# Attention's maxima in wider steps, and three scratch writes for four

## The chip, the cores and the metric

The kernel runs on one core of a Trainium2 chip. A core has five engines with their own instruction streams: TensorE (PE, matrix products and transposes into PSUM), VectorE (DVE), ScalarE (ACT), GpSimd (POOL) and SyncE (SP, which issues plain transfers). SBUF and PSUM are its two memories; sixteen DMA engines move data between SBUF and the chip's main memory. Indirect transfers (gathers of table rows by index) are issued from GpSimd's queue. The metric is the time of one execution on the device, in microseconds (us), as the median of several runs.

## The reference

A graph layer on 6250 nodes of 128 features and 200000 edges, sorted by their destination node. Everything is float32. `mesh_conv` gathers node rows, makes a message for every edge, and averages the messages by destination; attention follows:

```python
h = mesh_conv(x, src, dst, edge_attr, c1...)       # group norm, silu, segment mean
h = silu(group_norm(h)) + time embedding
h = mesh_conv(h, src, dst, edge_attr, c2...)
h = silu(group_norm(h)) + x
q, k, v = h @ qw + qb, h @ kw + kb, h @ vw + vb    # 8 heads of 16
logits = (q[dst] * k[src]).sum(-1) * scale + (edge_attr @ ew + eb)
amax = segment_max(logits, dst)
pe = exp(logits - amax[dst])
ssum = segment_sum(pe, dst)
o = segment_sum((pe / ssum[dst]) * v[src], dst)
return h + group_norm(o @ ow + ob)
```

## The kernel before

The edges are cut into 196 chunks of 1024 (eight tiles of 128 edges). There are three long stages: the two convolutions (`conv(1)`, `conv(2)`) and attention. Each walks the chunks once in `pipeline`, which writes out the order of the work. `in_order` pins that order on VectorE, ScalarE, TensorE and SyncE; GpSimd's order comes from its own issue order.

**Step n of attention's pipeline.** `fetch(n + 1)` issues the loads of the next chunk: SyncE loads the rows of the destination window (`pk`), and for every second chunk the positions from which the one-hot is made (`ohT`, 112 x 8 KB); GpSimd issues eight gathers (L622), one per tile, of 128 rows of keys and values (1 KB each) from `kv_d` into a buffer `g`. There are 11 such buffers. Then `second` finishes an older chunk, `first(n)` computes chunk n's logits, then some node work (`batch`, which finishes blocks of destination nodes that no further edge will touch) and `products(n + 1)`.

**First part.** `logits` multiplies the queries (`qe`, in PSUM, made by TensorE with the one-hot) with the gathered keys, tile by tile (L1187, three instructions), reduces over the head (L1190) and adds the edge term (L1192) into `lg`, which holds eight chunks.

**Maxima.** After eight chunks, a run, `maxima` makes the running maxima of the run. It is a generator with pieces, and between them the caller puts other work. Piece 1: transposes on TensorE of half of the logits (L1216, tile `lt`). Piece 2: the first forward scan on VectorE (L1219), then the transposes of the other half. Piece 3: the second forward scan, a backward scan over all 1024 edges (L1222), and transposes back (L1226, tile `rm`). Piece 4: the logits minus the maxima (L1230), the exponential on ScalarE (L1232), and eight products of the maxima with the end marks (L1234). The tiles `lt`, `rm` and the node work's `nd` share one place in PSUM.

**Second part.** For each chunk of the run before: the one-hot (`onehot`, L639), the late addition of the chunk before that into the table of sums (`add_late`, L1270 to L1276), the values weighted by the exponentials (`weighted`, L1244), the sums by destination on TensorE (`sums`, L1251), and `merge_late` (L1284 to L1262), which corrects the running maxima of the node windows. In the step in which a run has ended, the pieces of `maxima` stand between these; before the change: piece 1, one-hot, piece 2, late addition, piece 3, weighted product, sums, merge, piece 4, and then `first`.

**GpSimd's scratch writes.** After the eight gathers of a chunk, `gather` puts `REST[i]` memsets of a scratch tile `nst2` (128 x 392 elements, L634), which nothing reads: three in the convolutions, four in attention. The next chunk's gathers are issued behind them. Each gather also waits for the semaphore of the gather eight before it, and the first one of a chunk for its buffer.

Of the kernel before, what the change touches and what calls it, by code (L numbers as in the profile page):

```python
# [24 lines left out]
HD = 16  # L25
NT = 8
CH = NT * P
REST = {1: 3, 2: 3, 3: 4}
G = 8
GC = 2  # L30
BN = 4
# [14 lines left out]
def kernel(ctx: ExitStack, tc: tile.TileContext, x, src, dst, eat, w, out):  # L46
# [12 lines left out]
    NCH = EW // NT  # L59
# [538 lines left out]
    def loads(c, pools, rows_d, ahead):  # L598
        k = Chunk()
        k.c = c  # L600
        k.src, k.dm = src_i[:, c * NT:(c + 1) * NT], dm0[:, c * NT:(c + 1) * NT]
        if c == 0:
            load_group(0, pools)
        k.pk = pk[c % NPK]
        first = value(lo_i, c, SP, N - 1)
        nc.sync.dma_start(out=k.pk[:WN, :D], in_=rows_d[bass.ds(first, WN), :])
        g = c + (LG if ahead == 1 else 1)
        if g % LG == 0 and g < NCH:
            load_group(g, pools)
        k.ohT = pools[c // LG][:, c % LG, :]  # L610
        return k
# [8 lines left out]
    def gather(k, g, table_d, rest=0):  # L620
        def start(t):
            return nc.gpsimd.indirect_dma_start(  # L622
                out=g[:, t, :table_d.shape[1]], out_offset=None, in_=table_d,
                in_offset=bass.IndirectOffsetOnAxis(ap=k.src[:, t:t + 1], axis=0))

        with ExitStack() as es:
            if rested and rest:
                es.enter_context(tc.issue_after(rested.pop().ins))
            for t in range(NT):
                last = start(t)  # L630
        if rest:
            with tc.issue_after(last.ins):
                for _ in range(rest):
                    last = nc.gpsimd.memset(nst2, 0.0)  # L634
                rested.append(last)

    def onehot(k, pools, iota):
        k.oh = pools["oh"].tile([P, NT, P], FP, name="oh")
        return nc.vector.tensor_tensor(  # L639
            k.oh, iota[:, None, :].to_broadcast([P, NT, P]),  # L640
            k.dm[:, :, None].to_broadcast([P, NT, P]), ALU.is_equal)
# [322 lines left out]
    def conv(i):  # L964
# [4 lines left out]
        with ExitStack() as es:  # L969
# [73 lines left out]
            class Stage:  # L1043
# [4 lines left out]
                def fetch(self, c):  # L1048
                    k = loads(c, pools, a_d[i], self.ahead)
                    k.g = gp.tile([P, NT, D], FP, name="g")  # L1050
                    gather(k, k.g, b_d[i], REST[i])
                    k.h = hs[c % len(hs)]
# [5 lines left out]
                def first(self, k):  # L1058
                    if self.j == 0:
                        self.var = vp.tile([P, NV + BN * H], FP, name="var")  # L1060
                    k.reduce = first(k, self.var, self.j)
                    self.j += 1
# [60 lines left out]
            def left(k):  # L1123
                left_rows(k, pools, a_d[i], "m", [P, NT, D], 2)
                k.g = gp.tile([P, NT, D], FP, name="g")
                gather(k, k.g, b_d[i])
                k.h = hs[0]
                hidden(k, [(k.ohf.rearrange("p t e -> p (t e)"), k.rows[:, :D]), (k.ea, wcl)])
                var = vp.tile([P, NV + BN * H], FP, name="var")
                first(k, var, 0)()  # L1130
                nc.vector.reciprocal(rs_ps[:, :NT * H], deviations(NT * H, var)[:, :NT * H])
                k.rs = rs_ps[:, :NT * H]
                normed(k)
                summed(k)
                s = U[:, bass.ds(k.win, 1), :wide].rearrange("p o c -> p (o c)")
                nc.vector.tensor_tensor(s, s, k.u[:, :wide], ALU.add)
# [23 lines left out]
    with ExitStack() as es:  # L1160
# [21 lines left out]
        def logits(k, lg):  # L1182
            ebs = wk.tile([P, NT, H], FP, name="ebs")
            for a, qe in zip(range(0, NT, TB), k.qe):
                n = min(TB, NT - a)
                kk = k.g[:, a:a + n, :D]
                nc.vector.tensor_tensor(kk, qe[:, :n, :D], kk, ALU.mult)  # L1187
                nc.scalar.copy(ebs[:, a:a + n, :], qe[:, :n, D:])  # L1188
            l3 = wk.tile([P, NT, H], FP, name="l3")
            nc.vector.tensor_reduce(  # L1190
                l3, k.g[:, :, :D].rearrange("p t (h c) -> p t h c", c=HD), AX.X, ALU.add)
            nc.vector.tensor_tensor(lg, l3, ebs, ALU.add)  # L1192
# [46 lines left out]
        def weighted(k):  # L1239

            k.v = vp.tile([P, NT, VK + H + 1], FP, name="v")
            v4 = k.v[:, :, :VK].rearrange("p t (h c) -> p t h c", c=HD + 1)
            nc.scalar.copy(v4[:, :, :, HD], k.pe)
            nc.vector.tensor_tensor(  # L1244
                v4[:, :, :, :HD], k.g[:, :, D:].rearrange("p t (h c) -> p t h c", c=HD),
                k.pe[:, :, :, None].to_broadcast([P, NT, H, HD]), ALU.mult)

        def sums(k, wide):
            k.u = ps_.tile([P, 512], FP, name="u", tag="u", bufs=2)
            for t in range(NT):  # L1250
                nc.tensor.matmul(k.u[:, :wide], lhsT=k.oh[:, t, :], rhs=k.v[:, t, :wide],  # L1251
                                 start=(t == 0), stop=(t == NT - 1))
# [27 lines left out]
        def merge_late(k):  # L1280

            pres = k.u[:, VK + H:VK + H + 1]
            nm = wk.tile([P, 2], FP, name="nm")
            nc.vector.scalar_tensor_tensor(  # L1284
                nm, pres.to_broadcast([P, 2]), BIG, nm2[:, :, k.c], ALU.mult, ALU.add)
            cm = wk.tile([P, 2, H], FP, name="cm")
            nc.vector.tensor_tensor(
                cm, k.u[:, None, VK:VK + H].to_broadcast([P, 2, H]), nm[:, :, None].to_broadcast([P, 2, H]), ALU.add)
            k.win = value(w0_i, k.c, DVE, NW - 1)
            merge(k, M[:, bass.ds(k.win, 2), :], None, cm, 2)  # L1290

        def add_late(k):
            add(k, t3[:, bass.ds(k.win, 2), :], 2)

        class Stage:
            ahead = 1
            sums, late, nb = [], [], None
            lg, j = None, 0

            def __init__(self, bp):  # L1300
                self.bp = bp
# [3 lines left out]
            def fetch(self, c):  # L1305
                k = loads(c, pools, a_d[3], self.ahead)
                k.g = gp.tile([P, NT, KV], FP, name="g")
                gather(k, k.g, kv_d, REST[3])
                k.qe = []
# [5 lines left out]
            def first(self, k):  # L1315
                if self.j == 0:
                    self.lg = wk.tile([P, NT, G, H], FP, name="lg")
                logits(k, self.lg[:, :, self.j, :])
                self.j += 1

            def reduce(self, k):
                pass
# [5 lines left out]
            def second(self, run, ks):  # L1328


                pieces = iter(())
                if run:
                    pieces = maxima(run, self.lg, self.nb, self.bp)
                    self.nb, self.j = None, 0
                for n, k in enumerate(ks):
                    mine = pieces if n == len(ks) - 1 else iter(())
                    next(mine, None)
                    onehot(k, pools, iota)
                    next(mine, None)


                    if self.late:
                        add_late(self.late.pop(0))
                    next(mine, None)
                    weighted(k)
                    nc.scalar.copy(k.v[:, :, VK:VK + H], k.wl)
                    nc.scalar.copy(k.v[:, :, VK + H], ef[:, k.c * NT:(k.c + 1) * NT])
                    sums(k, VK + H + 1)
                    if self.sums:
                        merge_late(self.sums[0])  # L1350
                        self.late.append(self.sums.pop())
                    self.sums.append(k)
                for _ in pieces:
                    pass

            def batch(self, j):
# [95 lines left out]
```

## Time and profile before

| what | us |
|---|---|
| median of 3 runs (lowest to highest) | 7131.07 (7125.32 to 7133.75) |
| the profiled execution | 7126.42 |
| its span (first to last instruction) | 7124.6 |
| both convolutions, first to last gather | 56 to 4617 |
| attention, first to last gather | 4669 to 7051 |

The profile is of one execution. An engine's busy time is the sum of its instructions, without those that wait or only issue. A line of a group reads: line of the kernel, engine, operation, what is written from what, count, busy time, mean nanoseconds of one, and after the bar the idle time of the engine just before these instructions with what ended most of it ("issue" where nothing that the profile shows was waited for). In a timeline a line has the start, the length, the engine, the line and the operation; neighbours of one kind are merged, with their number, and the brackets hold the idle time before. In the table of stretches PEclk is the granted share of TensorE's clock.

### The profile page before, as it was taken

What the parts mean: (1) busy time and instruction counts of PE and PEld (TensorE: products, weight loads), DVE (VectorE), ACT (ScalarE), POOL (GpSimd) and SP (SyncE); (2) the same over time, 40 slices, a digit from 0 to 9 for tenths busy, and PEclk for the clock granted to TensorE, in tenths of its full rate; (3) what the DMA queues carried; (4) which work ended last, traced back from release to release, by engine and by line L of the source; (5) the groups of instructions that cost most, each with busy time, mean ns of one, the idle gap of its engine ahead of it and who ended that gap; (6) DMA issues with size and microseconds to landing.
All of it is one profiled execution on the core that took longest, in us unless ns stands there. A gap on an engine that the chain in (4) does not pass through costs nothing. (4 is left out here: it accounts for less than half of the span.)

```text
span 7124.6 us, 74065 instructions
## 1 busy us (share of the span) xinstructions
PE 3891.3 (55%) x20957; PEld 3685.5 (52%) x20958; DVE 5144.2 (72%) x7564; ACT 3308.5 (46%) x5293; POOL 5394.0 (76%) x6678
## 2 busy tenths in 40 slices
PE   5555555555555455555555555545555555555555
PEld 4555555555555455555555555535555555555554
DVE  7777777777777576667777777736667777777778
ACT  5555555555555555555555555522223333333332
POOL 5777777777777677777777777767777777777774
PEclk7776677777777666666777777767777777777777
DMA  5433333333333333333333333344455555555553
GB/s 148 117 97 91 94 110 92 100 100 100 95 100 89 91 90 94 95 94 89 101 107 106 100 106 106 86 130 132 131 146 140 141 142 140 141 146 141 138 139 89
DMA packets 414321, 800.44 MB, mean 112 GB/s; under 512 B 101813, under 2 KB 274984, under 8 KB 379496
## 3 DMA queue, kind: packets, MB, share of 16 engines
q0 software_dynamic: 175616, 411.34, 22.2%
q1 hardware_dynamic: 232646, 380.69, 19.0%
q10 hardware_dynamic: 5632, 3.51, 0.2%
q8 instruction: 172, 2.82, 0.2%
q14 instruction: 255, 2.09, 0.1%
HBM read 754.19 MB, written 40.96 MB: 112 GB/s over the span
## 5 line engine op out<-in xcount | busy, mean ns | idle before, releaser
L622 POOL DMA_INDIRECT g<-b_d,src_i x3136 | 3000.7, 957 | 978.7 <-issue 940.0
L1030 PE MATMUL u<-h,oh 128*128 128x129 f32 (+1 forms) x6272 | 1395.6, 412 | 1891.2 <-ACT h L1025 1891.2
L1030 PEld LDWEIGHTS u<-h,oh 128*128 128x128 f32 x6272 | 1290.1, 314 | 1971.5 <-ACT h L1025 1963.9
L622 POOL DMA_INDIRECT g<-kv_d,src_i x1568 | 1532.4, 977 | 500.9 <-issue 468.8
L1251 PE MATMUL u<-v,oh 128*128 128x145 f32 x3136 | 750.0, 425 | 767.2 <-DVE nm L1284 765.6
L1251 PEld LDWEIGHTS u<-v,oh 128*128 128x128 f32 x3136 | 698.5, 308 | 801.9 <-issue 801.9
L1000 PE MATMUL m<-pk,ohT 117*128 117x128 f32 x6272 | 973.7, 321 | 134.9 <-DVE h L1006 101.1
L1006 DVE TENSOR_TENSOR h<-m,g 128x1024 f32<-128x1024 f32 x392 | 479.0, 1222 | 762.3 <-DMA g<-b_d,src_i 750.4
L1000 PEld LDWEIGHTS m<-pk,ohT 117*128 117x128 f32 x6272 | 942.0, 237 | 162.1 <-DVE h L1006 126.9
L1025 ACT ACTIVATE h<-h 128x1024 f32<-128x1024 f32 x392 | 414.2, 1057 | 1182.9 <-DVE h L1024 1182.9
L634 POOL MEMSET nst<- 128x392 f32 x1960 | 842.7, 430 | 79.3
L1008 ACT ACTIVATE sq<-h 128x1024 f32<-128x1024 f32 x392 | 413.9, 1056 | 653.8 <-DVE h L1006 650.8
L1009 DVE TENSOR_REDUCE var<-sq 128x64 f32<-128x1024 f32 x392 | 477.7, 1219 | 314.8 <-ACT sq L1008 312.2
L1187 DVE TENSOR_TENSOR g<-qe,g 128x384 f32<-128x384 f32 (+1 forms) x588 | 293.8, 511 | 549.7 <-DMA g<-kv_d,src_i 510.1
L615 ACT ACTIVATE ohT<-ohT,minus_p 112x1024 f32<-112x1024 f32 x588 | 669.9, 1139 | 16.2 <-DMA ohT<-rel_d 16.0
L616 ACT ACTIVATE ohT<-ohT 112x1024 f32<-112x1024 f32 x588 | 621.4, 1057 | 18.7
L1178 PE MATMUL qe<-pk,ohT 117*128 117x136 f32 x3136 | 512.8, 319 | 165.5 <-ACT ebs L1188 159.3
L1178 PEld LDWEIGHTS qe<-pk,ohT 117*128 117x128 f32 x3136 | 474.1, 225 | 198.8 <-ACT ebs L1188 192.3
L1023 DVE TENSOR_TENSOR h<-h,cps 128x1024 f32<-128x1024 f32 x392 | 478.4, 1220 | 13.5
L1024 DVE TENSOR_TENSOR h<-h,cps 128x1024 f32<-128x1024 f32 x392 | 478.4, 1220 | 13.4
L1020 DVE TENSOR_TENSOR h<-h,cps 128x1024 f32<-128x1024 f32 x392 | 475.3, 1212 | 5.9
L639 DVE TENSOR_TENSOR oh<-cps,dm 128x1024 f32<-128x1024 f32 x392 | 475.9, 1214 | 0.0
(265 smaller groups left out, 4383.9 us busy)
## 6 DMA issues: line engine op xcount, KB each, us to landing
ohT<-rel_d SPq DMA_DIRECT2D x294, 896.0 KB
g<-b_d,src_i POOLq DMA_INDIRECT x3136
pk<-a_d SPq DMA_DIRECT2D x588, 56.0 KB
g<-kv_d,src_i POOLq DMA_INDIRECT x1568
ohT<-in_eat_dram SPq DMA_DIRECT2D x294, 40.0 KB
a_d<-n_o SPq DMA_DIRECT2D x28, 256.0 KB
kv_d<-n_o SPq DMA_DIRECT2D x28, 256.0 KB
n_h<-h_d SPq DMA_DIRECT2D x19, 256.0 KB
```

The source lines that it names most:

```text
L615: nc.scalar.activation(k.ohT[:WN, :], k.ohT[:WN, :], AF.Square, bias=minus_p[:WN])
L616: nc.scalar.activation(k.ohT[:WN, :], k.ohT[:WN, :], AF.Relu, bias=1.0, scale=-4.0)
L622: return nc.gpsimd.indirect_dma_start(out=g[:, t, :table_d.shape[1]], out_offset=None, in_=table_d, in_offset=bass.IndirectOffsetOnAxis(ap ...
L634: last = nc.gpsimd.memset(nst2, 0.0)
L1000: nc.tensor.matmul(k.m[:, t, :], lhsT=lhs[:, t * P:(t + 1) * P], rhs=rhs, start=(j == 0), stop=(j == len(terms) - 1))
L1006: nc.vector.tensor_tensor(k.mt, k.m, k.g, ALU.add)
L1009: return lambda: nc.vector.tensor_reduce(var[:, j * NT * H:(j + 1) * NT * H], sq.rearrange("p t (g c) -> p (t g) c", c=HD), AX.X, ALU.add)
L1023: nc.vector.tensor_tensor(k.mt, k.mt, over_edges(gam), ALU.mult)
L1024: nc.vector.tensor_tensor(k.mt, k.mt, over_edges(bet), ALU.add)
L1030: nc.tensor.matmul(k.u[:, :wide], lhsT=k.oh[:, t, :], rhs=k.h[:, t, :wide], start=(t == 0), stop=(t == NT - 1))
L1178: nc.tensor.matmul(qe[:, t, :], lhsT=lhs[:, e], rhs=rhs, start=(j == 0), stop=(j == len(terms) - 1))
L1251: nc.tensor.matmul(k.u[:, :wide], lhsT=k.oh[:, t, :], rhs=k.v[:, t, :wide], start=(t == 0), stop=(t == NT - 1))
```

## The change

Three things are changed, all in attention. The memsets after a chunk's gathers are three instead of four. The pieces of the maxima stand further apart: piece 2 comes after the late addition (before, ahead of it), and piece 3 after the sums (before, ahead of the weighted product). The last piece is kept and run by `first`, right behind the logits of the next chunk; for the very last run, which no chunk follows, it is run at once.

```diff
-REST = {1: 3, 2: 3, 3: 4}
+REST = {1: 3, 2: 3, 3: 3}
...
-            lg, j = None, 0
+            lg, j, pieces = None, 0, iter(())
...
             def first(self, k):
...
                 logits(k, self.lg[:, :, self.j, :])
                 self.j += 1
+                self.rest()
...
             def second(self, run, ks):
...
                     next(mine, None)
                     onehot(k, pools, iota)
-                    next(mine, None)
 
 
                     if self.late:
                         add_late(self.late.pop(0))
                     next(mine, None)
                     weighted(k)
...
                     sums(k, VK + H + 1)
+                    next(mine, None)
                     if self.sums:
                         merge_late(self.sums[0])
...
-                for _ in pieces:
+                self.pieces = pieces
+                if run and run[-1].c == NCH - 1:
+                    self.rest()
+
+            def rest(self):
+
+                for _ in self.pieces:
                     pass
```

The order that the program has after it, on VectorE, in the step in which a run ended: one-hot, late addition, first forward scan, weighted product, second forward scan, backward scan, merge, logits of the new chunk, subtraction L1230, the eight products L1234. On TensorE: transposes of the logits, sums, transposes back. On ScalarE the exponential stands behind the copies of the edge term. GpSimd's gathers are the same.

## The prediction

> **What bounds the kernel now.** I read the engine totals first, then the stage that the change touches, then who waits there.
>
> ```profile
> PE 3891.3 (55%) x20957; PEld 3685.5 (52%) x20958; DVE 5144.2 (72%) x7564; ACT 3308.5 (46%) x5293; POOL 5394.0 (76%) x6678
> ```
>
> No engine looks full. The busy sums of the two long stages (start, end, length; PE, PEld, DVE, ACT, POOL; clock, DMA share, GB/s) separate them:
>
> ```profile
> 56.00:4620.00 4564.00, 2508.09 (x13692) 2397.11 (x13691) 3329.58 (x3536) 2521.11 (x3121) 3510.90 (x4313) 0.72 0.37 99
> 4669.00:7051.00 2382.00, 1306.92 (x6804) 1216.58 (x6804) 1690.68 (x3749) 732.47 (x2045) 1866.27 (x2348) 0.72 0.51 139
> ```
>
> The second row is attention: POOL (GpSimd) is busy 78% and VectorE 71%. The grouped instructions of attention's middle, 5000 to 6800 us, say what POOL does in the rest:
>
> ```profile
> L622 POOL DMA_INDIRECT g<-kv_d,src_i x1181 | 1156.1, 979 | 365.4 <-issue 356.5 <-DVE g L1187 4.2 <-DVE wl L1234 3.3
> L634 POOL MEMSET nst<- 128x392 f32 x592 | 254.2, 429 | 25.6
> ```
>
> 1156.1 + 365.4 + 254.2 + 25.6 = 1801.3 us: the whole window. The idle part is 0.30 us ahead of each gather, put down to its own issue; buffers cost it some 9 us. The wait table of the same window has VectorE on the other side:
>
> ```profile
> DVE g L1187 <- DMA g<-kv_d,src_i: 353.9, 240, 4.2
> ```
>
> So gathers set the pace, and VectorE waits for them 354 us in 148 chunks, 2.4 us each. One period in the timeline of POOL:
>
> ```profile
> 5807.61 0.95 POOL L622 DMA_INDIRECT g<-kv_d,src_i  x1 [0.30 <-issue]
> ...
> 5817.30 1.89 POOL L634 MEMSET nst<- 128x392 f32 x4
> 5819.49 0.95 POOL L622 DMA_INDIRECT g<-kv_d,src_i  x1 [0.30 <-issue]
> ```
>
> 11.88 us from chunk to chunk: 8 gathers at 1.25 (10.0) and the four memsets with the issue after them (1.89). Nothing but POOL's own instructions is in it.
>
> **Part 1: one memset fewer.** A memset is 0.424 us and the gap to the next 0.058: 0.482 us a chunk. 196 chunks x 0.482 = 94.5 us. This is on the path as long as POOL waits for nothing. Three things could make it wait. (a) A free buffer: chunk 96's gather starts at 5831.38 into the buffer of chunk 85, whose last reader (L1244) ended at 5813.17, so 18.2 us are left; over all chunks in the trace the least is 13.7. (b) The landing of the gather eight before, since each gather waits for the semaphore of its slot. [...] The trace has 2.4 us for undisturbed gathers, but up to 7.9 from issue to landing where the one-hot's 896 KB load runs beside. [...] (c) VectorE: eight chunks take 8 x 11.89 + 2 = 97 us now and 91.3 after; VectorE waits for landings 19 us of each eight, so it needs 78 and keeps 13 over.
>
> The conv stages already run with three memsets, and their median period in the trace is 11.39 us, with gathers of 0.94 and memsets of 1.41 together. So POOL holds that period, though with rows half as long.
>
> Not all 196 pay. In the last chunks VectorE is late (chunk 190's products start 2 us after the last landing, 195's 6 us), so a faster gather there gives nothing: 6 chunks x 0.48 = 3 us, and a lead that it builds before that is spent there too; I take 6 us off, from 3 to 12.
>
> **Part 2: the scans move against the gathers.** The backward scan L1222 reads two SBUF operands. A gather that POOL starts inside it does not end until 0.76 us after it:
>
> ```profile
> 5838.70 2.28 DVE L1222 TENSOR_TENSOR_SCAN fw<-nbe,fw 64x1024 f32<-64x1024 bf16 x1
> 5838.88 2.86 POOL L622 DMA_INDIRECT g<-kv_d,src_i  x1 [0.30 <-issue]
> ```
>
> A gather that starts s us after the scan's start ends 3.04 us after that start, and loses 2.1 - s; one that started 0.05 us before a scan (at 5938.44, scan at 5938.49) took its usual 0.95. Of 26 scans 24 hit a gather, and their losses add up to 37.2 us. Memsets are not hit: at 7038.98 four of them take 1.88 us with a scan across them, and the gather behind them, 1.89 us into that scan, loses 0.2. [...]
>
> Where does the scan go? Now: one-hot, scan 1, late addition, scan 2, backward scan, weighted product. After: one-hot, late addition, scan 1, weighted product, scan 2, backward scan. One product (L1244 at 5840.90, the next start at 5842.02: 1.12 us) comes ahead of it. VectorE's clock is the landing of the chunk before, and POOL starts the next chunk 0.48 us earlier after that, so the scan falls 1.60 us later in the gathers' period: from 7.32 us (5838.70 - 5831.38) to 8.92. Gathers start at 8.75 and, after the memsets, at 11.41. The scan of 2.28 us then lies on the eighth gather's late part and on the memsets: no loss. Shifting all 26 scans by the same 1.60 leaves 10.8 us (8 of it in the first five runs, whose scans come earlier, at 6.5 to 7.0 us). Gain 26 us. But the eighth gather is only 0.17 us ahead: with a shift below 1.45 it is hit, and 29 to 35 us stay. Ends: 2 and 37; I take 26, since both terms are read from rows.
>
> **Part 3: the last piece behind the next logits.** The subtraction L1230 (0.68 us) and eight products L1234 (1.14 us) leave the stretch ahead of the landing and come after L1192; the exponential (0.60 us) goes with them on ScalarE. In that step VectorE is late by 1.0 to 2.3 us already; it becomes some 1 to 3 us later and starts the next step 1.8 us later. Behind it wait the next one-hot, the node work and, on TensorE, what uses the bank of the rm tile. VectorE's 2.4 us of slack per chunk takes it up in two steps; uncovered it would be 26 x 1.8 = 47 us. TensorE gains: the sums (4.2 us) run under the scans in place of waiting for the rm transposes, which had waited 4.45 us for L1222. On POOL's path: 0.
>
> **Part 4: node work's operations** (L795, L900, L902: all operands in SBUF, 0.69 us) cost gathers another 14.2 us now. The new period shifts them at random: 0, from -10 to +10.
>
> Sum: 94.5 - 6 + 26 = 114.5 us. The profiled execution had 7126.4 us (span 7124.6, so 1.8 lie around it), 4.7 below the median of the runs shown; 7131.1 - 114.5 = **7017 us**, 1.6% faster.
>
> **Rivals.**
> - *The scans still hit.* Only the memsets count: 94.5 - 6 - 2 = 86, **7045**. For it: a margin of 0.17 us. Against: none of the terms is guessed.
> - *The gain stops at VectorE or at landings.* If transfers crowd (51% of the DMA engines now, 53% after) and each landing comes later by most of the 0.48 us, POOL gains but VectorE gets its rows no sooner: 10 to 40 us, about **7105**. Against it: eighth gathers land 1.8 us after their end in nearly all chunks, with no growth within a chunk.
> - *Slower: VectorE becomes the bound.* Postponed pieces add waits on TensorE (the bank that lt, rm and nd share) until eight chunks take VectorE over 98 us. It decides from 19 us of added waits in each eight chunks; at 25 us a group of eight takes 104, and 24 groups x 6 us more give **7275**. Only 1.8 us is visible.
> - *Nothing happens*, if something not in the profile paces gathers and takes the memset's place: **7131**.
>
> **How the numbers follow.** The four parts as summed: 0.56 (own range 6995 to 7035). Scans still hit: 0.22. Stopped gain: 0.08, nothing: 0.03, slower: 0.11. About 0.2% (14 us) is what a measurement can tell from no change. Faster is 0.56 + 0.22 and 0.06 of the third: 0.84; same is 0.03 and the rest of the third: 0.05; slower 0.11. The range of 8 in 10 goes from 6985 (all 37 us won, node work better by 10) to 7095, which takes in the scans' rival with the larger tail loss and half of the stopped gain.
>
> **What would show it.** Right: POOL's timeline with three memsets of 1.41 us and 11.4 us from chunk to chunk; L622's mean for kv_d gathers near 0.95 in place of 0.979, L1222's start 0.1 to 0.3 us behind an eighth gather; VectorE's wait for gathers near 1.9 us a chunk. Wrong: L622's "issue" idle growing past 0.30, POOL waiting for L1244 or for a landing, gathers of 2 to 3 us beside L1222 still, or VectorE no longer waiting for gathers.

## The result and the profile after

| | before | after |
|---|---|---|
| median, us (lowest to highest) | 7130.9 (7125.32 to 7133.75), 4 runs | 7015.1 (7009.02 to 7021.43), 4 runs |
| ratio, with its 95% interval | | 0.9839 (0.9822 to 0.9856) |
| span of the profiled execution | 7124.6 | 7013.5 |
| first gather of attention starts | 4669.4 | 4671.8 |
| attention, first gather's start to last gather's end | 2381.7 | 2265.5 |
| from there to the end of the span | 73.5 | 76.1 |
| median period from chunk to chunk in attention | 11.892 | 11.415 |

The change saves 115.8 us of the median, and 7017 had been predicted. Of the 111.1 us in the span, attention gives 116.2, the tail takes back 2.6 and the convolutions, whose code is the same, 2.4.

This holds on the chip of this comparison and on one of the chips that the experiments ran on. On three others the kernel before takes 7327 to 7351 us. The changed kernel itself ran on one of these three and is 0.5% slower there; on the other two only parts and variants of it ran, and each of these with fewer than four writes is slower than the kernel before. The second half of the experiments is about that.

The engine totals of the changed kernel, as on the page:

```profile
PE 3856.5 (55%) x20957; PEld 3659.4 (52%) x20958; DVE 5143.7 (73%) x7564; ACT 3308.8 (47%) x5293; POOL 5285.4 (75%) x6482
```

POOL has 196 instructions fewer and 108.6 us less to do; VectorE's work is the same. The grouped instructions of attention's middle, 5000 to 6800 us, and VectorE's wait for gathers in that window (sum, count, longest):

```profile
L622 POOL DMA_INDIRECT g<-kv_d,src_i x1245 | 1195.8, 960 | 385.0 <-issue 369.7 <-DVE g L1187 6.9 <-DVE M L1262 3.0
L634 POOL MEMSET nst<- 128x392 f32 x468 | 201.8, 431 | 18.0
```

```profile
DVE g L1187 <- DMA g<-kv_d,src_i: 276.6, 212, 4.7
```

Gathers, memsets and the issue gaps again fill the whole window (1800.6 us), with 156 chunks in it for 148. The mean gather fell from 979 to 960 ns. The stalls, which are what gathers last beyond their usual 0.945 us, add up in this window to 10.4 us beside the backward scans (28.8 before) and 9.5 us beside other work (11.9 before). VectorE waits 1.77 us a chunk, where it waited 2.4 before. In the timeline of a step with the scans, the backward scan starts 0.31 us behind an eighth gather and lies across the memsets; none of them is longer for it:

```profile
5141.33 0.95 POOL L622 DMA_INDIRECT g<-kv_d,src_i  x1 [0.30 <-issue]
5142.59 0.94 POOL L622 DMA_INDIRECT g<-kv_d,src_i  x1 [0.30 <-issue]
5142.90 2.28 DVE L1222 TENSOR_TENSOR_SCAN fw<-nbe,fw 64x1024 f32<-64x1024 bf16 x1
5143.52 1.41 POOL L634 MEMSET nst<- 128x392 f32 x3
5145.23 0.95 POOL L622 DMA_INDIRECT g<-kv_d,src_i  x1 [0.30 <-DVE nm L1284]
```

### The profile page after: what moved, and what is told of

It reads as the page before. It is cut to its first block, busy times and chain, and to the rows that moved or that the text cites. A ratio compares the mean times of both kernels' runs of the same rounds, so it can differ in the third digit from the quotient of the medians.

```text
span 7013.5 us, 73893 instructions
## 1 busy us (share of the span) xinstructions
PE 3856.5 (55%) x20957; PEld 3659.4 (52%) x20958; DVE 5143.7 (73%) x7564; ACT 3308.8 (47%) x5293; POOL 5285.4 (75%) x6482
## 5 line engine op out<-in xcount | busy, mean ns | idle before, releaser
L622 POOL DMA_INDIRECT g<-kv_d,src_i x1568 | 1510.2, 963 | 500.9 <-issue 463.5
L1251 PE MATMUL u<-v,oh 128*128 128x145 f32 x3136 | 727.2, 415 | 755.7 <-DVE nm L1284 747.1
L1251 PEld LDWEIGHTS u<-v,oh 128*128 128x128 f32 x3136 | 675.1, 299 | 795.5 <-issue 795.5
L634 POOL MEMSET nst<- 128x392 f32 x1764 | 760.4, 431 | 67.9
```

What stands on the lines that cost most here:

```text
L622: return nc.gpsimd.indirect_dma_start(out=g[:, t, :table_d.shape[1]], out_offset=None, in_=table_d, in_offset=bass.IndirectOffsetOnAxis(ap ...
```

## The experiments

The experiments ran on four chips, here B to E, one after the other; A is the chip of the result above, of which no number is on record, so it may be C. Each kernel is compared with runs of the kernel before on its own chip. All versions do the whole computation.

| chip, kernel before (us) | version | median, us | ratio (95% interval) |
|---|---|---|---|
| A, 7130.9 | changed kernel | 7015.1 | 0.9839 (0.9822 to 0.9856) |
| B, 7351.3 | old pieces, three writes | 7501.6 | 1.0214 (1.0186 to 1.0241) |
| B | new pieces, four writes | 7341.3 | 0.999 (0.997 to 1.0009) |
| B | changed, last piece at once | 7384.6 | 1.0057 (1.0034 to 1.0079) |
| B | changed, no writes in attention | 7644.8 | 1.0403 (1.0379 to 1.0426) |
| C, 7132.2 | changed kernel | 7018.3 | 0.9841 (0.9825 to 0.9858) |
| C | old pieces, three writes | 7031.5 | 0.9859 (0.9843 to 0.9876) |
| C | changed, two writes | 6943.3 | 0.974 (0.9724 to 0.9756) |
| D, 7343.4 | changed, last piece at once | 7380.4 | 1.0059 (1.004 to 1.0078) |
| D | changed, one write | 7579.3 | 1.0321 (1.0276 to 1.0366) |
| D | changed, no writes in attention | 7631.2 | 1.0371 (1.0316 to 1.0426) |
| E, 7327.1 | changed kernel | 7361.0 | 1.005 (1.0025 to 1.0075) |

### One part at a time

The runs on chip B took the change apart. The write alone (the kernel before with three writes):

```diff
-REST = {1: 3, 2: 3, 3: 4}
+REST = {1: 3, 2: 3, 3: 3}
```

> One part alone: three memsets in attention, the pieces of the maxima where they were. Theory (GpSimd's instructions set the pace; a scan costs a gather 2.1 us less its offset): 196 x 0.48 = 94 us less, 6 lost in the tail; the scans move 0.48 us against the gathers, and the same shift of the 26 scans of before leaves 30 of their 37 us: 7036 us, chunk to chunk 11.41 us. Rival (the pieces carry the gain, the fourth memset hid behind something): within 30 us of 7131.

The pieces alone (the changed kernel with the fourth write back):

```diff
-REST = {1: 3, 2: 3, 3: 3}
+REST = {1: 3, 2: 3, 3: 4}
```

> The other part alone: the pieces apart, four memsets. Theory: the period stays at 11.89 us and the scans move 1.1 to 1.3 us, which leaves 27 to 31 of their 37 us: 7 to 10 us less, 7122 us. Rival (room between the pieces is what VectorE lacked): 30 us less or more, 7100 or below.

The changed kernel without the postponed piece:

```diff
                 self.pieces = pieces
-                if run and run[-1].c == NCH - 1:
-                    self.rest()
+                self.rest()
```

> The changed kernel, with the last piece of the maxima run at once behind the merge and ahead of the next logits, as before. Theory (VectorE's slack takes the last piece anywhere): 7015 us as changed, plus or minus 8, since only node work's place against the gathers moves. Rival (it must stand behind the logits, or VectorE's lateness reaches GpSimd): 26 x 1.8 = 47 us more, 7060.

And with no write in attention at all:

```diff
-REST = {1: 3, 2: 3, 3: 3}
+REST = {1: 3, 2: 3, 3: 0}
```

> The changed kernel with no memsets in attention. Theory: chunk to chunk 10.0 us; 196 x 3 x 0.48 = 282 us less, but each scan now hits a gather (26 x 1.5 = 39 us back from 18, so 20 lost), and VectorE needs 9.7 us a chunk, so some 20 to 40 us go in the tail: 6780 us. Rival (the memsets keep gathers from crowding something that the profile does not show): no gain below 7015, gathers that last over 0.95 us away from the scans, or waits of GpSimd for landings.

Only the pieces alone came out as expected in time: 10 us less, which the interval does not tell from no change. The reason given did not come out, as shown below, so the agreement is no support for it. Every version with fewer writes was slower than the kernel before; the version without writes missed its expectation by some 860 us. With a kernel before that was itself 3% slower than on chip A, the theory "GpSimd alone sets the pace" (theory A in what follows) had either fallen or was true on some chips only; theory B adds that TensorE has to deliver in time. So the changed kernel, the write alone and the kernel before (once, for its trace) ran on chip C, beside one step further:

> The changed kernel once more, beside the others of this call. Theory A, GpSimd alone paces attention: 110 to 120 us below the kernel before on the same chip, ratio near 0.984, whatever the chip. Theory B, GpSimd paces only as long as TensorE delivers in time: where the kernel before takes about 7130 us (granted clock near 0.723) the ratio is near 0.984; where it takes about 7350 us (granted clock near 0.694) the gain shrinks or turns, ratio 0.99 to 1.01, with VectorE waits for TensorE's results in attention and GpSimd waits for gather buffers, and attention takes 2300 to 2400 us for 2254.

> The old pieces with three scratch writes, once more. Theory A: 85 to 95 us below the kernel before, ratio near 0.987, on any chip. Theory B: near 0.987 where the kernel before takes about 7130 us; 1.015 to 1.03 where it takes about 7350 us, as in the first call. If it is slower on a chip where the kernel before takes about 7130 us, the cause lies in where the pieces stand and not in the chip.

> The kernel before, for its trace on the chip of this call. Theory A: chunk period of 11.9 us, attention 2370 us from the first gather to the last, GpSimd never waits for a buffer. Theory B: the same, since four scratch writes leave TensorE time; what waits for TensorE's results in attention stays under 20 us in sum even where the granted clock is near 0.69.

```diff
-REST = {1: 3, 2: 3, 3: 3}
+REST = {1: 3, 2: 3, 3: 2}
```

> The changed kernel with two scratch writes a chunk in attention for three. Theory A: another 0.48 us on 196 chunks, up to 94 us less than the changed kernel, of which the room of VectorE (78 busy of 91.3 us per eight chunks, now of 87.5) takes some: 20 to 90 us below it. Theory B: on a chip with a granted clock near 0.69 it is slower than the changed kernel by 20 to 150 us; near 0.72 it gains less than 40 us or loses.

On chip C the kernel before takes 7132 us (7135.7 in the profiled execution), and there theory A holds: the changed kernel gains 113.9 us, the write alone 100.7 (a little over the 85 to 95 expected, since it takes more of the scans' stalls away than expected), two writes 188.9. What the parts are worth there, from the traces (stalls as above; a scan's are those of the gathers that overlap it):

| | before | write alone | changed | two writes |
|---|---|---|---|---|
| median period, us | 11.902 | 11.420 | 11.418 | 10.927 |
| attention, us | 2386.8 | 2278.4 | 2263.9 | 2184.1 |
| stalls, scans', us | 39.3 | 28.6 | 14.8 | 28.8 |
| stalls, others', us | 16.8 | 13.3 | 12.6 | 13.1 |
| median start of the scan after its chunk's first gather, us | 7.30 | 8.04 | 9.07 | 9.60 |
| tail, us | 78.6 | 77.8 | 79.1 | 82.8 |

The write alone gives 0.482 x 195 = 94.0 us in the period and 14.2 in stalls; moving the pieces adds 14.5 us in attention (13.2 in the median). In the typical step of the write alone the scan starts inside the seventh gather and holds up the eighth:

```profile
5327.61 0.95 POOL L622 DMA_INDIRECT g<-kv_d,src_i  x1 [0.30 <-issue]
5328.11 2.28 DVE L1222 TENSOR_TENSOR_SCAN fw<-nbe,fw 64x1024 f32<-64x1024 bf16 x1
5328.86 2.29 POOL L622 DMA_INDIRECT g<-kv_d,src_i  x1 [0.30 <-issue]
```

The pieces alone, on chip B, put it 0.13 us ahead of the eighth gather's start in the step shown, and the gather takes 2.92 us, for 2.29 in the step above. 22 of 26 scans hit, and the stalls are 38.4 us, as much as in the kernel before (37.4 on A, 39.3 on C) and not the 27 to 31 us expected:

```profile
5533.66 2.28 DVE L1222 TENSOR_TENSOR_SCAN fw<-nbe,fw 64x1024 f32<-64x1024 bf16 x1
5533.79 2.92 POOL L622 DMA_INDIRECT g<-kv_d,src_i  x1 [0.30 <-issue]
```

So neither part alone moves the typical scan to where only memsets start inside it: the write moves it by 0.74 us in the median, the pieces by 1.30 (8.60 on B for 7.30 on C), and it takes both to pass the eighth gather's start at 8.77. With two writes the scan falls another 0.53 us later, the memsets are shorter (0.92 us in all for 1.41), and 24 of 26 scans hit gathers, most of them the next chunk's first ones. But the period follows the write, 0.49 us less, and that is worth more:

```profile
5312.52 0.95 POOL L622 DMA_INDIRECT g<-kv_d,src_i  x1 [0.30 <-DVE cm L1287]
...
5322.22 0.92 POOL L634 MEMSET nst<- 128x392 f32 x2
5323.44 0.95 POOL L622 DMA_INDIRECT g<-kv_d,src_i  x1 [0.30 <-DVE g L1187]
```

10.92 us from chunk to chunk, GpSimd waits for no buffer, and VectorE still waits for gathers (5000 to 6700 us, 221.1 us in some 152 chunks):

```profile
DVE g L1187 <- DMA g<-kv_d,src_i: 221.1, 157, 5.0
```

This version beats both kernels on chip C. It was not run on a chip like B.

### The other kind of chip

The runs on chips D and E asked how far the pace can go, and whether the postponed piece matters:

> The changed kernel with the last piece of the maxima put at once again behind the second parts, once more. Where the kernel before takes about 7130 us: theory A, the last piece's place is free on GpSimd's path, so as the changed kernel within 8 us, 7010 to 7026 us. The rival, that the place of the last piece carries a part of the gain (the next chunk's products of the logits then wait behind its 1.8 us and more): 20 to 60 us above the changed kernel. Where the kernel before takes about 7350 us: 1.003 to 1.008 times it, as in the first call.

```diff
-REST = {1: 3, 2: 3, 3: 3}
+REST = {1: 3, 2: 3, 3: 1}
```

> The changed kernel with one scratch write a chunk in attention. Where the kernel before takes about 7130 us: if GpSimd still sets the pace, 70 to 94 us below the 6943 us of two writes, 6850 to 6875 us; if VectorE (8.84 us busy a chunk, 10.9 us a chunk with two writes) or the landing of the gathers sets it by now, 6890 to 6945 us. Where the kernel before takes about 7350 us, slower than that by 1 to 4 per cent.

> The changed kernel without scratch writes in attention, once more. Where the kernel before takes about 7130 us: if GpSimd still sets the pace, 140 to 185 us below two writes, 6760 to 6800 us; if VectorE sets it, 6850 to 6945 us; if TensorE comes late as on the chip of the first call, 7100 us and above, with waits for TensorE's results in attention over 200 us in sum. Where the kernel before takes about 7350 us, 1.04 times it, as in the first call.

> The changed kernel once more. Where the kernel before takes about 7130 us: ratio 0.984, as measured twice. Where it takes about 7350 us (granted clock near 0.694), the two theories of that chip part: if the place of the last piece of the maxima is what keeps TensorE's answers in time, the changed kernel gains there too, ratio 0.985 to 0.99, 7235 to 7280 us, with a chunk period of 11.4 to 11.5 us in attention and under 20 us of GpSimd's waits for gather buffers. If three scratch writes are too few there wherever the pieces stand, it is like the version with the last piece at once, ratio 1.002 to 1.01, 7365 to 7420 us, with such waits of 60 us and more.

Chips D and E both turned out like B, so they confirm that kind (1.0059, 1.0321, 1.0371 for what had been expected of it) and leave open what one or no write does on a chip like A or C. Each chip was met in one stretch of time only, so whether it is the chip, or something else about that time, is not separated. On chip E the changed kernel itself is slower than the kernel before, by 34 us, nearly what was expected (7365 to 7420) if three writes are too few there wherever the pieces stand.

What differs is in the wait tables. The changed kernel on chip C, 4900 to 6900 us:

```profile
DVE g L1187 <- DMA g<-kv_d,src_i: 309.3, 220, 5.7
POOL g L622 <- DVE g L1187: 6.0, 20, 0.3
```

The same kernel and window on chip E ("remote" is a wait that no recorded instruction's end explains; the semaphore is TensorE's):

```profile
ACT v L1243 <- remote: 189.6, 53, 7.2
DVE fw L1219 <- remote: 105.5, 18, 9.0
DVE g L1187 <- remote: 96.0, 67, 4.2
DVE g L1187 <- DMA g<-kv_d,src_i: 73.6, 27, 7.0
POOL g L622 <- DVE v L1244: 44.7, 14, 3.3
POOL g L622 <- DVE cm L1287: 34.5, 30, 4.9
```

VectorE no longer waits mainly for gathers, but for TensorE, and GpSimd waits for buffers that VectorE has not given back. Chip C has no "remote" wait in this window. One such step of chip E's timeline:

```profile
5080.05 0.68 PE L1216 MATMUL lt<-ident,lg 128*64 128x128 f32 x4
...
5086.89 0.28 ACT L1243 COPY v<-pe 128x64 f32<-128x64 f32 x1 [7.19 <-remote]
5087.16 1.21 DVE L1219 TENSOR_TENSOR_SCAN fw<-nbs,lt 64x512 f32<-64x512 bf16 x1 [5.59 <-remote]
...
5089.76 0.95 POOL L622 DMA_INDIRECT g<-kv_d,src_i  x1 [3.31 <-DVE v L1244]
```

By the record the transposes end at 5080.73; the semaphore on which the scan waits does not move from 5076.91 to 5086.87, and then five times within 0.27 us. A gather starts 3.0 us late for it (3.31, less the usual 0.30). In all of attention 132 moves of this semaphore come less than 0.1 us behind another on chip E; on A and C no two are closer than 0.43 us. (On E the trace holds 726 such moves for 855 matmuls that should make one, on A and C 864 to 868 for 868 at most, so some are missing there.) All seven kernels with three writes or fewer that ran on B, D and E show these waits on "remote" and bunched moves, and the sum of GpSimd's waits in attention (gathers after the first that start over 0.2 us later than usual) grows as writes are taken away: 84 us for the changed kernel (E), 100 and 115 with the last piece at once (B, D), 265 for the old pieces with three writes (B), 515 with one write (D), 643 and 618 with none (B, D). With four writes (B) it is 6.5, as on A and C, though 52 moves of the semaphore are bunched there too, and VectorE waits for gathers again (4900 to 6900 us):

```profile
DVE g L1187 <- DMA g<-kv_d,src_i: 366.8, 258, 8.0
DVE g L1187 <- remote: 3.2, 2, 2.4
```

On such a chip the moved pieces matter at three writes: on chip B the write alone takes 7501.6 us, and 7384.6 us once pieces 2 and 3 are moved as well, with GpSimd's waits at 100 us for 265. So 117 us of what the write alone costs there come back, while with four writes the pieces bring nothing clear of noise.

Where the changed kernel's gain goes on chip E can be counted against the version with four writes (chip B), since no trace of the kernel before was taken on such a chip. The period is 11.470 for 11.920, so 0.45 x 195 = 88 us should be gained; GpSimd's waits take back 84.4 - 6.5 = 78, and the backward scans' stalls are 41.7 us for 38.4, which leaves 7 us by this count; measured, attention is 2376.6 for 2388.1. Nothing of the scans' gain is left on chip E: 23 of 26 scans hit gathers, most of them the second gather of a later chunk, as in the step above:

```profile
5090.84 2.28 DVE L1222 TENSOR_TENSOR_SCAN fw<-nbe,fw 64x1024 f32<-64x1024 bf16 x1
5091.02 2.86 POOL L622 DMA_INDIRECT g<-kv_d,src_i  x1 [0.31 <-issue]
```

The tail is 112.9 for 76.5, since VectorE ends attention some 36 us behind. In sum 25 us worse; the medians on chip E differ by 34.

The place of the last piece is worth little there: attention takes 2376.6 us with it postponed (E), 2404.4 and 2394.8 at once (D, B), but the ratios are 1.005, 1.0059 and 1.0057, and their intervals overlap. On a chip like A or C it was not taken alone.

## Why the prediction was right, and where it was not

**The bound, and Part 1 (94.5 less 6).** Right on chips A and C. The period falls by 0.477 us on A, 93.0 us over 195 periods, and by 0.484 on C, 94.4. GpSimd waits for no buffer and no landing (6.5 us in all of attention beyond its usual gaps, as before). The tail takes 2.6 us on A and 0.5 on C, less than the 3 to 12 allowed. The version with two writes shows that VectorE had the room estimated for it: at 10.93 us a chunk it still waits 1.45 us a chunk for gathers.

**Part 2 (26, ends 2 and 37).** Right in mechanism on A and C, too large on A: the scans' stalls fall from 37.4 to 18.2 us on A (19.2) and from 39.3 to 14.8 on C (24.5). The eighth gather ahead of the scan, whose margin of 0.17 us was the doubt, is the lesser matter: a typical scan starts 0.3 us behind it. The loss is at the other end. The typical shift is 1.77 us and not 1.60 (medians of 7.33 and 9.10 us), and in some runs of chunks the scan comes 0.5 to 2.1 us later still, past the memsets onto the next chunk's first gathers; the first run on either chip and the first four of 26 on A are hit earlier in the chunk. Twelve of 26 scans on A cost nothing, the others 0.3 to 2.0 us each. The prediction made the shift of both parts, 1.12 us from the product and 0.48 from the earlier gathers; on C, 10.7 us of the fall come with the write alone, and on B the pieces alone bring none.

**Part 3 (0 on GpSimd's path)** agrees with the sum on A and C, which leaves nothing over for it, and was not isolated there.

**Part 4 (0, within 10).** The other stalls fall by 3 us on A (14.0 to 11.0) and by 4 on C: inside the ends.

**The sum.** On A: 93.0 + 19.2 + 3.0, and 1.0 of small gaps, is attention's 116.2; less the tail and the convolutions' 2.4 it is the span's 111.1, and 115.8 in the medians, for 114.5 predicted. That the two come within 1.3 us is partly luck: Part 2 was 6.8 us too large, the tail's loss 3.4 us too large and Part 4 3.0 us too small, and the profiled execution of the kernel before lies 4.5 us below its median.

**The rivals.** "The scans still hit" holds for 14 of 26 scans on A, at half their former cost. "The gain stops at VectorE or at landings" fell on C, where the next write removed is worth 75 us more. "Slower" does not occur on A or C; on E the chain that it names does, VectorE behind TensorE and GpSimd behind VectorE, at +34 us and not +144. But its cause was sought in the postponed pieces, and the runs of B and D show it with the last piece at once, and in the old order, too; on B, at three writes, it is worst in the old order.

**What the prediction had no term for** is what differs on chips B, D and E. "POOL waits for nothing" was worked out from one trace of one chip, with margins of 13.7 us for buffers and 13 us in eight chunks for VectorE. It left out how late TensorE's answers can come, because in that trace nothing waits on "remote".

## What to carry to other kernels

When an idle instruction is all that paces a producer, taking it away pays its own length per round (0.482 us a chunk here, and the period fell by 0.477 on A and 0.484 on C) only while every consumer has room, and that room has to be measured on more than one chip: here one write less is worth 1.4% on one chip and costs 2.1% on another, in the old order of the pieces. Where two engines disturb each other (a gather that started inside the backward scan took 2.29 to 2.92 us in the steps shown, for 0.95), work out the phase of one in the other's period for each part of a change and for their sum; here neither part alone moved the typical scan clear of the gathers, and together they did, on the chips where nothing else moved it.

## What the runs showed that was not expected

On chips B, D and E the kernel before takes 2.8 to 3.1% longer than on A. The version with four writes, nearest to it among the traces from there, starts attention at 4847.7 us for 4669.4: most of what is lost lies ahead of attention, where ScalarE waits hundreds of us on "remote" at L1036:

```profile
ACT uw L1036 <- remote: 468.4, 129, 9.5
```

The kernels on A and C wait 6.4 to 6.7 us in all there. The convolutions have three writes in every version; whether a fourth would help them on such a chip was not run. The mean granted clock of TensorE in the traces is 0.687 to 0.704 on those chips and 0.723 to 0.738 on A and C.

TensorE's answers come well after the recorded end of its matmuls there (6.1 us for the transposes of the step shown; VectorE waits up to 9.0 us on "remote" in the changed kernel's attention), in stretches where the record of the granted clock reads full or half speed (half from 5066.5, full from 5080.2, half from 5083.6 us around the step shown). Two readings of this are open: matmuls that ended later than recorded, and answers that were ready and reported late. The bunched moves of the semaphore speak for the second: in the step shown five come within 0.27 us, some 0.07 us apart, while no two recorded ends of matmuls that move it are under 0.43 us apart. No run here tells the two readings apart, and the recorded ends are modelled, so why the answers are late on these chips, and why a faster GpSimd makes them later, stays open. That four writes keep attention in step there (11.92 us a chunk) and three do not (medians of 11.42 and 11.47 us, with 265 and 84 us of GpSimd's waits) is shown; that the writes act by giving TensorE time is only argued, and so is it of the moved pieces.
